# Perceiver megakernel: both products of the self-attention's values in one step, right ahead of the context's weighted values

## The chip, the cores and the metric

The kernel runs on one core of a Trainium2 chip. The metric is the device time of one execution in microseconds (us). The kernel before takes 2138.94 us (median of 3 runs, 2138.63 to 2139.02).

TensorE (PE) does the matrix products into PSUM, VectorE (DVE) and ScalarE (ACT) read PSUM and do the elementwise work and reductions, GpSimd (POOL) works on SBUF alone, and SyncE (SP) issues nearly all DMAs. Each engine takes its instructions in order, and an instruction that waits holds up what stands behind it.

## The reference, cut to what matters

The input is x (32 batches x 64 rows x 256) and a context (32 x 1601 x 256). Two layers follow each other, each of cross attention, a mixer and a feed-forward part, each with a layer norm ahead and a residual sum behind:

```
x = x + L0_xattn(ln(x), ctx)     # a mean of the context, two matmuls
x = x + L0_attn(ln(x))           # self-attention over 64 rows, 16 heads of 16, with a slope per head
x = x + L0_ffn(ln(x))            # shared expert + 2 of 8 routed experts
x = x + L1_xattn(ln(x), ctx)     # 16 heads over 1601 context rows: nearly all of the work
x = x + L1_attn(ln(x))           # convolution, a recurrent unit, a feed-forward part
x = x + L1_ffn(ln(x))            # ternary weights, quantised activations
```

The change is in L0_attn:

```
scores = q @ k.T / sqrt(16) + slopes * dist
attn   = softmax(scores)         # 64 x 64 for each batch and head
ctx    = attn @ v
out    = ctx @ Wo.T + bo
```

## The kernel before, in words

**Tiles.** The 2048 rows of x are 16 tiles of 128 rows (two batches each), taken in the order 1, 2, ..., 15, 0. The first layers (the three L0 steps) of a tile are one Python generator, `layer0`; the second cross attention is the main loop; what comes behind it for a tile is another generator, `tail`.

**The main loop** runs over `g`, 13 iterations for each tile: 12 pieces of 512 context columns (2 batches x 2 halves of the heads x 3 pieces) and one for the 65 columns left in each batch. For each `g` the engines' instructions are written in this order, which is also the order in which each engine's queue gets them:

1. `column_scores(g)`: the scores (PE lines 816 and 822, tile `s`), and their exp on ACT into `pt` (line 828).
2. `values(g + 4)`: values of the context (PE line 234 into `vps`, copied by DVE into `vau`, line 758). Once for each piece row also `maxima_rows` (`tpm`, line 797).
3. `run(g, 0)`: the planned generators' steps that were announced with `yield ACT`.
4. `row_scores(g + 5)`: scores by rows (PE line 774, tile `r`) and their maxima on DVE (line 781).
5. `weighted(g)`: the context's weighted values (PE line 846, tile `o` from `pt` and `vau`), matmuls of 128 rows and 32 columns each.
6. `keys(g + 6)`: keys (PE line 234 into `kps`, copied by ACT into `kt`, line 741).
7. `run(g, 1)`: the planned generators' other steps.

**The planner.** `Steps` holds a generator with a start, an end and a number of steps. With `place=3` it takes at most one step at each place of an iteration, and only as far as its due time allows; a step announced with `yield ACT` goes to place 0, any other to place 1. The first layers of the tiles 4 to 15 and 0 are planned in this way, two tiles overlapping. Tile 3 has `place=2` (any step at either place), tile 2 runs beside the start of the loop, and tile 1 is issued ahead of the loop, step by step from a list.

**The self-attention's end in `layer0`.** After the softmax, with the weights in `s`, there are three steps, all at place 0 of successive iterations:

- first: `weights(0)` turns four pairs of heads by TensorE transposes (line 416, PSUM tile `tpp`), and `weights_out` copies them to `pT` on ACT (line 421);
- second: `weights(1)`, then `summed_values(0, pT)`: eight matmuls of 128 rows and 32 columns (line 428; 16 records in the trace) into a PSUM tile `o0`, and ACT's copy with a bias to `oT` (line 431); then the second copy into `pT`, whose tag has one buffer;
- third: `summed_values(1, pT)`.

The output projection `wo` (line 234) and the residual sum follow at place 1, then `tp_c`, `su`, `sv`, `lg` and `so` of the shared expert.

**PSUM.** `s` and `r` share two tiles of two banks each, so `r` waits for the exps and the next `s` for the maxima. All other matmuls (`vps`, `kps`, `tpm`, and every step of the generators) take turns in three buffers of one bank (`mm_tile`), in the order in which they are written.

Of the kernel before, what the change touches and what calls it, by code (L numbers as in the profile page):

```python
# [15 lines left out]
P = 128  # L16
# [28 lines left out]
def perceiver_kernel(ctx: ExitStack, tc: tile.TileContext, a: dict, out: bass.AP):  # L45
# [14 lines left out]


    ACT = "ACT"

    def sc_tile(name):
        return ps_sc.tile([P, 2, 512], F32, tag="sc", name=name)
# [225 lines left out]
    def layer0(ti, csum, k=0, soon=False):  # L291
        def tile_(shape, tag, name):
            return front_tile(shape, tag, f"{name}_{ti}", k)
# [16 lines left out]
        xn = normalised(tile_([P, D], "xn", "xn_a"), m)  # L310
        yield ACT
        xT = transposed(xn, f"a{ti}", SECOND["xT"] if k else "xT")
# [21 lines left out]
        xn = normalised(tile_([P, D], "xn", "xn_b"), m)  # L334
        yield ACT


        xT = transposed(xn, f"b{ti}", SECOND["xT"] if k else "xT")
        yield ACT
        q_ps = mm_tile([P, 2, P], f"q0_{ti}")  # L340
# [11 lines left out]
        kbd = [tile_([P, 2, 4, S], "kbd", f"kbd{oc}") for oc in range(2)]  # L352
        for oc in range(2):
            nc.gpsimd.tensor_tensor(  # L354
                kbd[oc], kT[:, oc, :].rearrange("p (b k) -> p b k", b=2).unsqueeze(2).to_broadcast([P, 2, 4, S]),
                mask4.unsqueeze(1).unsqueeze(3).to_broadcast([P, 2, 4, S]), ALU.mult)
        yield ACT
        v_ps = mm_tile([P, 2, P], f"v0_{ti}")
# [40 lines left out]
        else:  # L399
            nc.gpsimd.tensor_tensor(s, s, mx.unsqueeze(2).to_broadcast([P, H, S]), ALU.subtract)  # L400
            yield
            yield ACT
            nc.scalar.activation(s, s, AF.Exp)
# [4 lines left out]
            yield  # L408
            yield ACT
        oT = tile_([P, 2, P], "oT", "oT")  # L410

        def weights(oc):
            t = mm_tile([P, 4, P], f"tpp_{ti}_{oc}")
            for j in range(4):
                hp = 4 * oc + j
                nc.tensor.transpose(t[:, j, :], s[:, 2 * hp:2 * hp + 2, :].rearrange("p h k -> p (h k)"), ident)
            return t

        def weights_out(oc, t):
            pT = tile_([P, 4, P], "pT", f"pT{oc}")  # L420
            nc.scalar.copy(pT, t)
            return pT

        def summed_values(oc, pT):
            o_ps = mm_tile([P, P], f"o0_{ti}_{oc}")
            for b in range(2):
                for i in range(4):
                    nc.tensor.matmul(o_ps[32 * i:32 * i + 32, b * S:(b + 1) * S],
                                     lhsT=vbd[k][:, b, 4 * oc + i].rearrange("p h d -> p (h d)"),
                                     rhs=pT[:, i, b * S:(b + 1) * S], start=True, stop=True)  # L430
            nc.scalar.activation(oT[:, oc, :], o_ps, AF.Identity, bias=chv[:, oc, BV:BV + 1])

        pT = weights_out(0, weights(0))
        yield ACT
        t = weights(1)
        summed_values(0, pT)
        pT = weights_out(1, t)
        yield ACT
        summed_values(1, pT)
        yield  # L440
        o = mm_tile([P, D], f"wo_{ti}")
        mm2(o, lambda c: oT[:, c, :], lambda c: w_o[:, c, :])
# [250 lines left out]
    def scanned(g):  # L693

        pos, p = divmod(g, NU)
        return (pos, 4 * pos + (p - 1) // NP, (p - 1) % NP) if p else (pos, None, None)
# [86 lines left out]
    def maxima(h):  # L783

        hf = halves[h]
        ng = small.tile([P, 4], F32, tag="ng", name=f"ng_{hf.name}")
        nc.vector.tensor_reduce(ng, wholes[hf.pos].mx[:, :, h % 4, :], AX.X, ALU.max, negate=True)
        m = mxp[h % 2]
        nc.vector.tensor_copy(m[:, :, 0], ng)
        nc.vector.tensor_tensor(ng, ng, m[:, :, 0], ALU.subtract)  # L790
        nc.vector.tensor_copy(m[:, :, 1], ng)
        nc.vector.tensor_tensor(m[:, :, 2], ng, m[:, :, 1], ALU.subtract)
# [38 lines left out]
    def weighted(g):  # L831

        pos, h, k = split(g)
        w = wholes[pos]
        first, last = g % NU == 0, g % NU == NU - 1
        if first:
            w.o = o_tile([P, 4, 2, S], f"o1_{w.ti}")
        v, pts = vau[g % 5], w.pt.pop(g)
        kr = TAIL if h is None else P
        for j in range(4):  # L840
            q = j if h is None else h % 4
            for m in range(2):
                for c in range(4):
                    hd = 4 * m + c

                    nc.tensor.matmul(w.o[32 * c:32 * c + 32, q, m, :], lhsT=v[:kr, j, 17 * hd:17 * hd + 32],  # L846
                                     rhs=pts[m][:kr, c // 2, j, c % 2 * S:c % 2 * S + S],
                                     start=(m == 0 and (first and j == 0 or h is None and j == 3)), stop=(m == 1 and (last and j == 3 or h is None and j == 2)))
        if h is None:
            w.osb = work.tile([P, 2, 4, S], F32, tag="osb", name=f"osb_{w.ti}", bufs=1)  # L850
            nc.vector.tensor_copy(w.osb[:, :, 0:3], w.o[:, 0:3].rearrange("p q m s -> p m q s"))
        elif last:
            nc.vector.tensor_copy(w.osb[:, :, 3], w.o[:, 3])
# [307 lines left out]
    class Steps:  # L1161
# [14 lines left out]
                    self.gen = None  # L1176

        def run(self, t, place):
            at = place if self.place == 2 else self.place
            if self.place == 3:  # L1180
                if (self.kind == ACT) != (place == 0):
                    return
                at = place
            if at == place:
                now = t + (0.5 * place if self.place >= 2 else 0)
                while self.gen is not None and self.done * (self.t1 - self.t0) <= (now - self.t0) * self.n:
                    self.step()
                    if self.place == 3:
                        break
# [85 lines left out]
    with tc.manual_schedule(engines={ET.PE, ET.DVE, ET.Activation, ET.Pool}):  # L1275
        ahead, beside, summing = Steps(first()), Steps(first_layer(1, 1)), Steps(early_sums())

        def besides():
            if 1 in csums:
                beside.step()  # L1280

        def scored():
            row_scores(scores.pop(0))

        scores = list(range(5))
        do = {"a": ahead.step, "b": besides, "s": summing.step, "r": scored, "w": late_weights, "m": lambda: maxima(0),
              "t": lambda: maxima_rows(0)}
        do |= {f"k{g}": lambda g=g: keys(g) for g in range(6)} | {f"v{g}": lambda g=g: values(g) for g in range(3)}

        for what in """a a a a k1 a a k2 a a s s k3 k0 a a a a s s s s a k4 a v0 v1 a a a s s s s s s b a b a b a b a s w  # L1290
                    a s s a a a b a a s s s r b r b s s s r k5 b r m s s s r v2 t""".split():
            do[what]()
        if beside.gen is not None:
            plan.insert(0, Steps(beside.gen, 0, 4, 28 - beside.done, 2))
        planned(biased(), 3, 5, 2, 1)
        if summing.gen is not None:
            plan.insert(0, Steps(summing.gen, 0, 4.5, 37 - summing.done, 0))
        planned(all_ternary(), 5, 23, 24, 2)

        def run(t, place):  # L1300
            for s in [s for s in plan if s.t0 <= t]:
                s.run(t, place)
                if t >= s.t1 and t < NU * NT - 1:
                    s.all()
                if s.gen is None:
                    plan.remove(s)

        for g in range(NU * NT):
            pos, p = divmod(g, NU)
            if pos + 1 < NT:  # L1310
                if p == 0:
                    wholes[pos + 1].rest = load_rest(order[pos + 1])
                if p in (2, 9):
                    load_batch(2 * pos + 2 + p // 8)
            column_scores(g)
            if g == 0:
                values(3)
            if g + 4 < NU * NT:
                values(g + 4)
            if p == 1 and pos:  # L1320
                normalise(pos - 1)
            if g + 4 < NU * NT and scanned(g + 4)[2] == NP - 1:
                maxima_rows(scanned(g + 4)[1])
            run(g, 0)
            if g + 5 < NU * NT:
                row_scores(g + 5)
                if scanned(g + 5)[2] == NP - 1:
                    maxima(scanned(g + 5)[1])
            weighted(g)
            if p == NU - 1:  # L1330
                gathered(pos)
            if g + 6 < NU * NT:
                keys(g + 6)
            if p == 1 and pos:
                x4[pos - 1] = projected(pos - 1)
            run(g, 1)
        normalise(NT - 1)
        x4[NT - 1] = projected(NT - 1)
        plan.append(Steps(second_layer(NT - 1)))
        while plan:  # L1340
            for s in list(plan):
                s.step()
                if s.gen is None:
                    plan.remove(s)
# [46 lines left out]
```

## Time and profile before

| what | value |
|---|---|
| median of 3 runs | 2138.94 us |
| the profiled execution, its time | 2137.64 us |
| its span | 2135.9 us |
| TensorE busy | 2020.8 us (95%) |
| VectorE, ScalarE, GpSimd busy | 1296.5, 906.4, 324.1 us |
| products of values, L428 | 512 records, 37.1 to 1563.6 us |
| transposes, L416 | 128 records, 35.0 to 1554.9 us |
| copies pT, L421, on ACT | 32, median 585 ns |
| copies oT, L431, on ACT | 32, median 367 ns |

A matmul in float32 is two records in the trace. In a timeline, a line is a run of like instructions: start, length in us, engine, line of the kernel, operation, out<-in, sizes and count, and in brackets the idle time before it and what ended it. Ends of matmuls are modelled and reach into the next run, so the time that a run holds TensorE is read from its start to the start of the next. In the chain a line is start, length, and what ran. In the answer on one line of the kernel, a row names what TensorE sat idle for, the sum in us and how many times.

### The profile page before, as it was taken

Reading aid. Unit: us, or ns where it says so; the run is one execution under the profiler, and the core shown is the slowest. Engines: PE = TensorE matmul, PEld = TensorE weight load, DVE = VectorE, ACT = ScalarE, POOL = GpSimd, SP = SyncE. Lnnn points to the kernel's source line nnn. Section 1 sums busy time; section 2 is a strip of 40 time slices with the busy share of each in tenths; the row PEclk is TensorE's granted clock in tenths of the full one; section 3 lists DMA queues with packets and bytes.
Section 4 is the critical chain, followed back from the end, with each engine's and each line's share of the span. In section 5 each row is a group of like instructions: output and inputs, shape, how many; then the busy total and the mean of one; then the engine's idle time right before and its main releaser. Section 6 shows DMA issues by size and latency. Waiting matters only on the chain.

```text
span 2135.9 us, 69475 instructions
## 1 busy us (share of the span) xinstructions
PE 2020.8 (95%) x31675; PEld 1468.0 (69%) x31675; DVE 1296.5 (61%) x2607; ACT 906.4 (42%) x1402; POOL 324.1 (15%) x538
## 2 busy tenths in 40 slices
PE   5899999999999999999999999999999999999964
PEld 3566677777776777777777777767776666676753
DVE  4555756666656666665667666566666656565544
ACT  4344444543546343444544434343433334334332
POOL 2121211111111111111111111111200111000011
PEclk9899999999999999999999999999999999999986
DMA  8334322221222212112211101111111111101000
GB/s 301 101 107 149 111 93 95 81 84 36 95 80 86 89 43 76 38 58 72 70 59 38 48 9 45 38 38 43 45 45 34 50 38 35 55 2 45 2 14 5
DMA packets 54638, 136.37 MB, mean 64 GB/s; under 512 B 13318, under 2 KB 34760, under 8 KB 54344
## 3 DMA queue, kind: packets, MB, share of 16 engines
q1 hardware_dynamic: 53784, 131.12, 18.1%
q8 instruction: 248, 4.06, 0.8%
q10 hardware_dynamic: 560, 0.81, 0.1%
q14 instruction: 46, 0.38, 0.1%
HBM read 125.60 MB, written 6.32 MB: 62 GB/s over the span
## 4 chain that ended last, share of the span: by engine, by line
PE 86%; DVE 8%; ACT 3%; issue 2%; DMA 1%; POOL 1%; SPq 0%; POOLq 0%; DVEq 0%; ACTq 0%
PE vps L234 18%; PE kps L234 16%; PE r L774 10%; PE o L846 9%; PE s L822 8%; PE ff L234 4%; PE s L816 3%; DVE mx L781 3%; PE ffo L997 2%; PE q L234 1%; PE wo L234 1%; ACT pt L828 1%; DVE vau L758 1%; PE hg L948 1%; PE h L1046 1%
## 5 line engine op out<-in xcount | busy, mean ns | idle before, releaser
L781 DVE TENSOR_REDUCE mx<-r 128x2 f32<-128x1024 f32 x384 | 451.8, 1219 | 123.1 <-PE r L774 122.8
L828 ACT ACTIVATE pt<-s 128x1024 f32<-128x1024 f32 (+1 forms) x416 | 403.1, 1020 | 276.5 <-PE s L822 276.3
L741 ACT ACTIVATE kt<-kps,chv 128x512 f32<-128x512 f32 x192 | 131.9, 687 | 641.6 <-PE kps L234 641.6
L234 PE MATMUL kps<-ctxT,w_L_xattn_WkT 128*128 128x512 f32 x768 | 384.2, 623 | 11.8 <-DMA ctxT<-ctxT 11.8
L234 PE MATMUL vps<-w_L_xattn_WvT,ctxT 128*128 128x128 f32 x3072 | 393.5, 281 | 1.3 <-DVE y L923 0.7
L234 PEld LDWEIGHTS vps<-w_L_xattn_WvT,ctxT 128*128 128x128 f32 x3072 | 357.4, 191 | 26.4 <-issue 3.8
L758 DVE COPY vau<-vps 128x512 f32<-128x512 f32 (+1 forms) x208 | 143.3, 689 | 355.6 <-PE vps L234 355.3
L846 PEld LDWEIGHTS o<-pt,vau 128*32 128x32 f32 (+1 forms) x13312 | 195.6, 110 | 150.8 <-issue 138.2
L846 PE MATMUL o<-pt,vau 128*32 128x64 f32 (+1 forms) x13312 | 230.0, 221 | 5.3 <-ACT pt L828 5.2
L774 PE MATMUL r<-kt,qbd 32*128 32x512 f32 x1536 | 227.6, 645 | 2.8 <-DVE mx L781 2.0
L234 PEld LDWEIGHTS kps<-ctxT,w_L_xattn_WkT 128*128 128x128 f32 x768 | 131.4, 191 | 124.1 <-issue 106.9
L822 PEld LDWEIGHTS s<-qbd,kt 32*128 32x128 f32 x6144 | 205.4, 186 | 3.0
L822 PE MATMUL s<-qbd,kt 32*128 32x128 f32 x6144 | 206.8, 270 | 0.0
L774 PEld LDWEIGHTS r<-kt,qbd 32*128 32x128 f32 x1536 | 65.5, 184 | 39.8 <-issue 19.0
L816 PE MATMUL s<-neg,onesb 3*128 3x512 bf16 x768 | 80.8, 384 | 5.1 <-DVE mx L781 4.1
L816 PEld LDWEIGHTS <-onesb 3*128 3x128 bf16 x768 | 21.0, 90 | 93.5 <-issue 91.9
L276 ACT ACTIVATE part<-part 128x1601 f32<-128x1601 f32 x48 | 74.1, 1544 | 0.2
L234 PE MATMUL ff<-nT,w_fg 128*128 128x128 f32 x384 | 51.7, 287 | 1.0 <-ACT nT L984 1.0
L234 PEld LDWEIGHTS ff<-nT,w_fg 128*128 128x128 f32 x384 | 47.9, 200 | 1.9 <-ACT nT L984 1.8
L354 POOL TENSOR_TENSOR kbd<-kT,mask 128x512 f32<-128x512 f32 x32 | 32.6, 1041 | 108.0 <-ACT kT L347 108.0
L234 PE MATMUL ff<-nT,w_fv 128*128 128x128 f32 x384 | 48.9, 278 | 0.0
L400 POOL TENSOR_TENSOR s<-s,mx 128x1024 f32<-128x1024 f32 x15 | 28.6, 1904 | 118.6 <-DVE mx L384 118.2
(339 smaller groups left out, 2444.5 us busy)
## 6 DMA issues: line engine op xcount, KB each, us to landing
ctxT<-ctxT SPq DMA_DIRECT2D x31, 1601.0 KB
part<-ctxT SPq DMA_DIRECT2D x60, 800.5 KB
od<-osb SPq DMA_DIRECT2D x16, 256.0 KB
rest<-ctxT SPq DMA_DIRECT2D x32, 65.0 KB
x<-x SPq DMA_DIRECT2D x16, 128.0 KB
rs<-od SPq DMA_DIRECT2D x32, 64.0 KB
og<-od SPq DMA_DIRECT2D x32, 64.0 KB
out<-x SPq DMA_DIRECT2D x16, 128.0 KB
```

Of the source, the lines that this page charges most:

```text
L234: nc.tensor.matmul(o, lhsT=lhsT(c), rhs=rhs(c), start=(c == 0), stop=(c == 1))
L276: nc.scalar.activation(parts[j], parts[j], AF.Copy, accum_out=csum[:, c, 2 * i + b:2 * i + b + 1])
L354: nc.gpsimd.tensor_tensor(kbd[oc], kT[:, oc, :].rearrange("p (b k) -> p b k", b=2).unsqueeze(2).to_broadcast([P, 2, 4, S]), mask4.unsqueez ...
L741: nc.scalar.activation(kt, o, AF.Identity, bias=chv[:, hf.oc, BK2:BK2 + 1])
L758: nc.vector.tensor_copy(v[:kr, :, 0:VW - 16].rearrange("p k (h d) -> p k h d", d=17)[:, :, :, 0:16], o[:kr].rearrange("p k (h d) -> p k h ...
L774: nc.tensor.matmul(o, lhsT=qbd[r, q % 2, q // 2].rearrange("p h q -> p (h q)"), rhs=w.kt[r, q, :] if h is None else halves[h].kt[k][r, :], ...
L781: nc.vector.tensor_reduce(w.mx[:, 2 * m:2 * m + 2, h % 4, k], ps[m], AX.X, ALU.max)
L816: nc.tensor.matmul(o, lhsT=onesb[r, :], rhs=halves[h].neg[r, :].unsqueeze(1).to_broadcast([3, 4, P]), start=True, stop=False)
L822: nc.tensor.matmul(ps[i // 2][:kr, i % 2, j * P:(j + 1) * P], lhsT=w.kt[r, j, :] if h is None else halves[h].kt[k][r, j * P:(j + 1) * P], ...
L828: nc.scalar.activation(pt[:kr].rearrange("p i k c -> p i (k c)"), ps[m][:kr], AF.Exp)
L846: nc.tensor.matmul(w.o[32 * c:32 * c + 32, q, m, :], lhsT=v[:kr, j, 17 * hd:17 * hd + 32], rhs=pts[m][:kr, c // 2, j, c % 2 * S:c % 2 * S ...
L997: nc.tensor.matmul(o, lhsT=m[:, f, :], rhs=w_fo[:, f, :], start=(f == 0), stop=(f == NF - 1))
```

## The change

Both products move into one step of their own, behind both steps of transposes. A new kind of announcement, `COL`, has its step run at a new place, 0.5, between `row_scores` (with `maxima`) and `weighted`. Generators planned with `place=2` have no place 0.5 and take the step at place 0 or 1. The second copy of the weights no longer shares the buffer of the first: it takes one of the two buffers of the tag `kbd`, which also hold the masked keys and, later, the routed experts' weights.

```
-            pT = tile_([P, 4, P], "pT", f"pT{oc}")
+            pT = tile_([P, 4, P], ("pT", "kbd")[oc], f"pT{oc}")
...
-        pT = weights_out(0, weights(0))
-        yield ACT
-        t = weights(1)
-        summed_values(0, pT)
-        pT = weights_out(1, t)
-        yield ACT
-        summed_values(1, pT)
+        pT = [weights_out(0, weights(0))]
+        yield ACT
+        pT.append(weights_out(1, weights(1)))
+        yield COL
+        for oc in range(2):
+            summed_values(oc, pT[oc])
         yield
...
         def run(self, t, place):
-            at = place if self.place == 2 else self.place
+            at = place if self.place == 2 and place != 0.5 else self.place
             if self.place == 3:
-                if (self.kind == ACT) != (place == 0):
+                if {ACT: 0, COL: 0.5}.get(self.kind, 1) != place:
                     return
                 at = place
...
                     maxima(scanned(g + 5)[1])
+            run(g, 0.5)
             weighted(g)
```

More of the change, by code (lines that the diff above doesn't have):

```diff
@@ L62, in perceiver_kernel @@
     ACT = "ACT"
+    COL = "COL"
     def sc_tile(name):
```

## The prediction

> **What bounds the kernel now.** The page was read first: busy times and the rows of 40 slices, then the chain.
>
> ```profile
> PE 2020.8 (95%) x31675; PEld 1468.0 (69%) x31675; DVE 1296.5 (61%) x2607; ACT 906.4 (42%) x1402; POOL 324.1 (15%) x538
> PE 86%; DVE 8%; ACT 3%; issue 2%; DMA 1%; POOL 1%; SPq 0%; POOLq 0%; DVEq 0%; ACTq 0%
> ```
>
> TensorE is busy 95% of the span and carries 86% of the chain. The busy times by stretch say where it idles:
>
> ```profile
> 120.00:1560.00 1440.00, 1415.81 (x22903) 1035.92 (x22902) 903.78 (x1797) 652.82 (x1006) 239.87 (x369) 1.00 0.20 67
> ```
>
> Between 120 and 1560 us, where all but three tiles' first layers run, it is busy 1415.81 of 1440 us at a granted clock of 1.00. So the change is worth what it does to TensorE's own queue, read from start to start in the timeline. Below is tile 15: first the iteration with its second group of transposes and its first product of values, then the next one with its second product.
>
> ```profile
> 1441.09 0.60 PE L416 MATMUL tpp<-ident,s 128*128 128x128 f32 x4
> 1441.62 0.43 PE L428 MATMUL o<-pT,vbd 128*32 128x64 f32 x16
> 1441.98 1.14 PE L774 MATMUL r<-kt,qbd 32*128 32x512 f32 x8
> 1443.05 1.10 PE L846 MATMUL o<-pt,vau 128*32 128x64 f32 x64
> 1444.08 1.98 PE L234 MATMUL kps<-ctxT,w_L_xattn_WkT 128*128 128x512 f32 x4
> ...
> 1449.10 0.22 PE L797 MATMUL tpm<-identb,mxp 128*128 128x128 bf16 x1
> 1449.25 0.43 PE L428 MATMUL o<-pT,vbd 128*32 128x64 f32 x16
> 1449.61 1.14 PE L774 MATMUL r<-kt,qbd 32*128 32x512 f32 x8
> ```
>
> What to see: a product (16 matmul records, each with a weight load that moves with it) holds the queue 0.36 us from its start to that of the row scores r. The context's weighted values (L846) have the same shape, 128x64 out of weights of 128*32, and hold it 1.03 us for 64 records, 0.016 us each. A product alone pays 0.022 us a record, as a short run pays the change into r each time.
>
> **The change, part by part.** Durations are of the profiled execution: span 2135.9 us, its time 2137.64 us, 1.3 us under the median of 2138.94 us.
>
> *Thirteen steady tiles (4 to 15, and 0).* In the changed kernel's order of instructions both products stand between r and L846, in the iteration of the second transposes. They leave two places.
> First place: transposes to product is 0.53 us, and transposes straight to r takes the same (a tile's first transposes, 1324.53 to 1325.06), so 0.36 us goes. Second place: from tpm to product 0.15 us, from tpm to r 0.14 us (1571.80 to 1571.94): another 0.36 us goes. Added: 32 records ahead of 64 of their own shape. L846 without its exit (0.15 us, the gap between its last start and the next line's) is 0.88 us for 63 steps, so 32 steps cost 0.45 us; r to a product should cost what r to L846 does, 1.07 us. Net 0.45 - 0.72 = -0.27 us, times 13 = **-3.5 us**. Bounds: 0, if the merged run keeps 0.36 us a product, and -0.36 us a tile, if one product rode along free. I take the row of the same shape in the same place.
> In seven of the 13, a step of full 128x128 size (tp_a in six, tp_b in one) stands right behind the second product. From the last start of the context's value product (vps) to the first of a product it is 0.20 us in the trace, to a full-size step 0.11 us; the dearer entry goes: 7 x 0.09 = **-0.6 us**.
>
> *Waits that go.* Beyond the 0.53 us, the first product starts late by 0.73 us in tiles 8 and 0, 0.20 in tiles 5 and 13, 0.09 in tiles 10 and 12; the second by 0.19 and 0.10 in tiles 9 and 10; tp_a behind it is late by 0.28, 0.41, 0.18, 0.28 in tiles 6, 9, 11, 14. What they wait for, from the answer on the product's line after 120 us:
>
> ```profile
>   DVE rr L953: 2.9, 4
>   DVE vau L758: 2.3, 6
> ```
>
> (TensorE and its weight loads each counted.) Both are readers of an older tile in the three shared PSUM buffers. Behind r the products start 1.07 us later, when those readers are through, and a product no longer pushes tp_a onto the buffer that vau is being copied from. Sum 3.5 us, less 0.1 each in tiles 8 and 0 for the next point: **-3.3 us**; bounds 0 (they return at another step) and -3.5.
>
> *The wait that is added.* The second product now needs pT1, whose transposes are in the same iteration.
>
> ```profile
> 1439.37 1.94 ACT L828 ACTIVATE pt<-s 128x1024 f32<-128x1024 f32 x2 [0.60 <-PE s L822]
> 1442.12 0.37 ACT L431 ACTIVATE oT<-o,chv 128x128 f32<-128x128 f32 x1 [0.80 <-PE o L428]
> 1442.38 0.58 ACT L421 COPY pT<-tpp 128x512 f32<-128x512 f32 x1
> ```
>
> Today pT1 stands behind oT0 on ACT; after the change it stands ahead of it, and ACT is idle 0.80 us there. The transposes end at 1441.69; pT1 would run 1441.75 to 1442.33. The second product is due 0.53 + 1.07 + 0.22 us after 1441.09, at 1442.91: 0.5 us in hand. Behind a late one L846, keys and the next s would stand. ACT is later than that in tiles 8 and 0 (a tanh of L952 ahead: 0.1 us) and in tile 9.
> Tile 9: the second exp ends at 790.01 only, and r cannot pass it, so its first place gives back nothing; with a Square ahead of pT1 I read 0.3 us above the formula. The exps also bind where little is left between values and r: behind a lone tpm, r takes longer,
>
> ```profile
> 1571.94 1.25 PE L774 MATMUL r<-kt,qbd 32*128 32x512 f32 x8
> ```
>
> 0.12 us above its 1.14. Tiles 7, 15 and 0 become such: 0.36. Together **+0.7 us**.
>
> *The first three tiles.* Tile 1 lies on the chain, where TensorE is idle and latency counts:
>
> ```profile
> 37.18 0.41 PE o L428 x16
> 37.60 0.37 ACT oT L431
> 37.97 0.48 ACT pT L421
> 38.50 0.43 PE o L428 x16
> ```
>
> pT1 no longer waits for the buffer of pT0 and for oT0. Transposes end at 37.18, pT1 runs 37.25 to 37.83, the second product starts at 37.87 instead of 38.50: -0.6. Tile 2: the product's wait for pT0 (105.55 to 106.06) leaves the path, 0.24 us of product comes in behind keys: -0.3. Tile 3: transposes to xat fall from 0.95 us (174.12 to 175.07) to 0.44, 0.24 comes in behind the next values: -0.3. **-1.2 us**; bounds -0.6 and -1.5.
>
> *At nothing.* ACT runs the same copies in another order; in tiles 4, 7 and 10 a part sum (L276, 1.53 us) stands between pT1 and oT0, covered by L846 and keys (1.03 + 1.92 us) before the output projection wants oT. POOL's second kbd write now waits for the previous tile's second product instead of its scores; it follows 10 us or more later (275.2 to 285.5 at the closest). On SP the first four w13 loads move behind a rest, a context load and an output; they wait for the last tile's product near 1557 instead of issuing at 1510.25, are wanted at 1633.9, and the next issue behind them is at 1575.70. The steps after the product (wo, tp_c, su, lg, so) come one iteration earlier in most tiles. Their own instructions are the same, but they meet other tiles' steps. No row prices that; iterations with three or more tiles behind the value product fall from 85 to 80 in the order, single waits of this kind are 0.2 to 0.5 us: bounds -1.5 and +2, taken as 0.
>
> **Sum:** -3.5 - 0.6 - 3.3 + 0.7 - 1.2 = -7.9 us. 2137.64 becomes 2129.7; against the median, 2138.94 - 7.9 = **2131.0 us**, 0.37% faster. About 0.2% (4.3 us) can be told from no change here.
>
> **The rivals.**
> *The waits move elsewhere.* Buffers stay three, and the later steps meet new neighbours; then the 3.3 goes and up to 2 comes: -4.6 to -2.6, 2134 to 2136. For: a third tile behind values is still there 80 times. Against: the removed ones sit at the product itself. 18%.
> *The merged run keeps the price of two single ones.* 32 records cost 0.72, the steady gain is nil: -7.9 + 3.5 = -4.4, 2134.5. Against: L846's 64 records in 1.03 us. 10%. [...]
> *Slower: pT1 late.* The product waits in order, with L846 behind it. If one more ACT task of a part sum's length (1.53 us) ran ahead of pT1 in each of the 13 tiles, it would cost 1.53 - 0.5 = 1.0 us a tile against a gain of about 0.55 (the 3.5, 0.6 and 3.3 over 13): +6, 2137.64 - 1.2 + 0.7 + 6 = 2143 in the profiled execution, 2144 by the median. It decides from 1.05 us of delay on. Against: in the changed order part sums stand behind pT1, and only L952 and Square come ahead, in few tiles. 8%.
> *The change doesn't do what it says*, the products being held to a later iteration by the planner's pace: all 13 stand in the iteration of their transposes, so it has no chance.
> New neighbours that also remove waits: 4%.
>
> **How the numbers follow.** The sum as told has 60%, its own range 2127.5 to 2134.5. The bounds added up reach from -11.1 to about +1.5, 2127.8 to 2140.4; the range 2127 to 2138.5 leaves out the late pT1 and the ends. Faster by over 0.2% (under 2134.7): nearly all of the 60, the 4, half of the 10 and half of the 18, less a little for what was not seen: 0.75. Same: 0.16. Slower 0.09.
>
> **What would show it.** After the change: L428 as one run of 32 records between r and L846, together 1.5 us; transposes to r 0.53 us; no wait of L428 for rr or vau; pT1 ahead of oT0 on ACT, and the product waiting for pT1 only in tiles 8, 9 and 0; the start of tile 1's projection 0.6 us earlier; TensorE busy a few us less. Wrong would be: r to L428 far above 1.07 us, waits for pT in most tiles, or new waits at tp, su or wo for vau that add up to more than 3 us.

## The result and the profile after

| | before | after |
|---|---|---|
| median | 2138.79 us (2137.12 to 2139.61, 6 runs) | 2127.99 us (2126.34 to 2129.98, 6 runs) |
| ratio, with its 95% interval | | 0.9949 (0.9940 to 0.9959) |
| span of the profiled execution | 2135.9 us | 2125.2 us |

The change makes the kernel 0.51% faster: 10.8 us by the medians, 10.7 us by the spans of the two profiled executions. The forecast was 7.9 us. Lines of the kernel after are numbered two higher than before up to the product's step, and one higher from there on: the product is L430, the transposes L418, the copies pT L423 and oT L433, r L775, the weighted values L847. In most of the experiments the lines behind the product's step are 6 or 7 higher still; a tile's name tells which step a row is.

The page of the kernel after, busy times and the chain by engine:

```profile
PE 2014.4 (95%) x31659; PEld 1468.2 (69%) x31675; DVE 1298.1 (61%) x2607; ACT 906.4 (43%) x1402; POOL 325.2 (15%) x538
PE 86%; DVE 8%; ACT 2%; issue 1%; DMA 1%; POOL 1%; SPq 0%; POOLq 0%; DVEq 0%; ACTq 0%
```

The busy times by stretch, the same stretch as before (length, then busy time and count of TensorE, its weight loads, DVE, ACT and POOL; granted clock; DMA share; GB/s):

```profile
120.00:1560.00 1440.00, 1420.06 (x23087) 1043.11 (x23094) 912.71 (x1814) 657.65 (x1012) 240.79 (x371) 1.00 0.20 67
```

TensorE is still what bounds the kernel. In the same 1440 us it is busy 4.25 us more and gets through 184 matmul records more (23087 against 22903), at the same granted clock of 1.00. The gain is in TensorE's queue, as the forecast said, and shows as more work done in the stretch.

Tile 15 in the timeline of the kernel after, TensorE:

```profile
1430.34 0.60 PE L418 MATMUL tpp<-ident,s 128*128 128x128 f32 x4
1430.87 1.14 PE L775 MATMUL r<-kt,qbd 32*128 32x512 f32 x8
1431.94 0.65 PE L430 MATMUL o<-pT,vbd 128*32 128x64 f32 x32
1432.41 1.08 PE L847 MATMUL o<-pt,vau 128*32 128x64 f32 x64
1433.42 1.12 PE L236 MATMUL kps<-ctxT,w_L_xattn_WkT 128*128 128x512 f32 x2
```

From start to start: transposes to r 0.53 us, r to the product 1.07, the product's 32 records 0.47, the weighted values 1.01. Before, the two products held the queue 0.36 us each and the weighted values 1.03.

ACT in the same iteration:

```profile
1428.63 1.94 ACT L829 ACTIVATE pt<-s 128x1024 f32<-128x1024 f32 x2 [0.60 <-PE s L823]
1430.98 0.58 ACT L423 COPY pT<-tpp 128x512 f32<-128x512 f32 x1 [0.41 <-PE tpp L418]
1432.44 0.62 ACT L433 ACTIVATE oT<-o,chv 128x128 f32<-128x128 f32 x2 [0.88 <-PE o L430]
```

The second pT now stands ahead of both oT copies and ends at 1431.56, 0.38 us before the joined run starts.

What TensorE waited for between 120 and 1560 us (sum in us, times, longest). The main rows of before that are gone or smaller after:

```profile
PE o L428 <- DVE rr L953: 1.2, 2, 0.6
PE q L234 <- ACT kT L347: 0.7, 1, 0.7
PE tp_a L218 <- DVE vau L758: 0.7, 3, 0.3
PE tp_b L218 <- DVE vau L758: 0.5, 1, 0.5
PE tp_b L218 <- ACT xT_d L224: 0.5, 2, 0.2
PE v L362 <- ACT xT_c L224: 0.5, 1, 0.5
PE o L428 <- DVE vau L758: 0.3, 1, 0.3
```

and the rows of after that are larger than before, new, or what is left of those above:

```profile
PE r L775 <- ACT pt L829: 3.8, 9, 0.5
PE vps L236 <- issue: 0.6, 1, 0.6
PE tp_a L220 <- DVE vau L759: 0.3, 1, 0.3
```

The product of values waits for nothing any more in this view. Three of the rows that went (q, v, and tp_b for xT_d) are not waits of the product or of the step behind it: they belong to steps further down, and the forecast had no term for them. Three more rows of before, of 0.3 to 0.5 us each, went as well, and two small ones came: wo for oT, 0.3 us, and tp_c for xn_c, 0.2 us, once each.

Where along the run the time goes is read by comparing the two timelines iteration by iteration, each from the start of its first matmul to the start of the next iteration's. The shift of after against before is -1.14 us at the end of iteration 17 (the first three tiles), -11.66 at the end of iteration 161 (the thirteen steady tiles), still -11.66 at iteration 203, and -10.66 at the end. So the steady tiles gave 10.5 us, the first ones 1.1, and the last stretch took 1.0 back. That last loss is the clock's: the granted clock was 0.83 and 0.74 between 2034 and 2042 us (the last section).

### The profile page after: what moved, and what is told of

The parts are those of the page before. It is cut to its first block, busy times and chain, and to the rows that moved or that the text cites. A ratio compares the mean times of both kernels' runs of the same rounds, so it can differ in the third digit from the quotient of the medians.

```text
span 2125.2 us, 69448 instructions
## 1 busy us (share of the span) xinstructions
PE 2014.4 (95%) x31659; PEld 1468.2 (69%) x31675; DVE 1298.1 (61%) x2607; ACT 906.4 (43%) x1402; POOL 325.2 (15%) x538
## 4 chain that ended last, share of the span: by engine, by line
PE 86%; DVE 8%; ACT 2%; issue 1%; DMA 1%; POOL 1%; SPq 0%; POOLq 0%; DVEq 0%; ACTq 0%
PE vps L236 18%; PE kps L236 16%; PE r L775 10%; PE o L847 9%; PE s L823 8%; PE ff L236 4%; PE s L817 3%; DVE mx L782 3%; PE ffo L998 2%; PE q L236 1%; PE wo L236 1%; ACT pt L829 1%; PE hg L949 1%; PE h L1047 1%; PE gps L633 1%
## 5 line engine op out<-in xcount | busy, mean ns | idle before, releaser
L847 PEld LDWEIGHTS o<-pt,vau 128*32 128x32 f32 (+1 forms) x13312 | 196.6, 110 | 141.6 <-issue 129.1
L847 PE MATMUL o<-pt,vau 128*32 128x64 f32 (+1 forms) x13312 | 230.4, 221 | 5.3 <-ACT pt L829 5.2
L775 PE MATMUL r<-kt,qbd 32*128 32x512 f32 x1536 | 227.8, 645 | 2.8 <-DVE mx L782 2.0
L775 PEld LDWEIGHTS r<-kt,qbd 32*128 32x128 f32 x1536 | 65.6, 184 | 41.4 <-issue 21.7
L236 PEld LDWEIGHTS ff<-nT,w_fv 128*128 128x128 f32 x384 | 46.1, 194 | 0.0
```

What stands on the lines that cost most here:

```text
L236: nc.tensor.matmul(o, lhsT=lhsT(c), rhs=rhs(c), start=(c == 0), stop=(c == 1))
L775: nc.tensor.matmul(o, lhsT=qbd[r, q % 2, q // 2].rearrange("p h q -> p (h q)"), rhs=w.kt[r, q, :] if h is None else halves[h].kt[k][r, :], ...
```

## The experiments

In all of them but the one that moves the place itself, the tiles 1, 2 and 3 are as in the change; diffs are against the changed kernel, and in those with an `else:` the lines shown stand in it, for the tiles 4 to 15 and 0. Two kinds of number are given. The median goes with a ratio to the kernel before, timed along with the experiment. The steady shift is worked out from the traces: the shift against before at the end of iteration 161 less that at the end of iteration 17. It leaves out the start, where profiled executions differ by up to 4.4 us ahead of the steady tiles; in the change it is -10.52 us. It still holds differences of single executions: iterations 113 and 139, whose order is the same in the change and in the run with the place one step later, differ there by 0.4 and 0.2 us. The expectations call the account of the forecast, with the iteration of the later steps as a cause of its own, A; their other letters are rivals that lay the gain on fewer causes.

### One step at place 0: the joined products, without the new place

```
-            yield COL
+            yield ACT
             for oc in range(2):
                 summed_values(oc, pT[oc])
```

The joined products run at place 0 in the iteration after the second transposes, where the second product was; all later steps keep their old iterations.

> Both products in one step, but at place 0 (ahead of the row scores) of the iteration behind the second transposes, so that the later steps stay in the iterations they had before; tiles 4 to 15 and 0 only, the first three tiles as in the change. Theory A (the gain of 10.8 us is about 1 us from the first three tiles, 6 us from the place of the products and 4 us from the later steps coming one iteration earlier): one of two changes of shape remains, -0.36 + 0.22 us a tile, 13 x -0.14 = -1.8, the waits at the first product go, -2, and 1 from the first tiles: about 2134. Theory B (all of it is the place between row scores and weighted values): only the first tiles' 1 us is left, 2138. Theory C (all of it is the earlier iteration): 2138 too.

Measured: 2139.04 us, ratio 0.9994 (0.9985 to 1.0004): no gain, about 5 us above the expected 2134; steady shift +0.80 us. The miss is in the second place. The first place gave back its 0.36 us in nearly all tiles, and 1.04 in tiles 8 and 0, as expected; but the joined run held the queue far longer than expected, for instance in tile 15, in this run's timeline:

```profile
1452.00 0.22 PE L804 MATMUL tpm<-identb,mxp 128*128 128x128 bf16 x1
1452.15 0.43 PE L430 MATMUL o<-pT,vbd 128*32 128x64 f32 x16
1453.04 0.43 PE L430 MATMUL o<-pT,vbd 128*32 128x64 f32 x16 [0.46 <-DVE vau L765]
1453.40 1.14 PE L781 MATMUL r<-kt,qbd 32*128 32x512 f32 x8
```

1.25 us from the first product to r, where one product alone held 0.36. The second product takes a second of the three PSUM buffers at once, close behind the values' own. In four tiles (6, 7, 14, 15) it waits until DVE has copied `vau` out of one, in two (9, 10) for ACT, and in three others the step behind it waits for `oT`. Where nothing waits (tiles 5, 13 and 0) the joined run holds 0.58 to 0.59 us, as expected. The waits view of this run gives the sums (one more row is 0.3 us for `qT_i`):

```profile
PE o L430 <- DVE vau L765: 1.3, 4, 0.5
PE o L430 <- ACT h L1047: 0.9, 1, 0.9
PE tp_a L220 <- ACT oT L433: 0.5, 2, 0.3
PE tp_b L220 <- ACT oT L433: 0.3, 1, 0.3
```

What follows: joining the products was worth nothing here, where no other long step stands between the values and them. I had counted the buffers for the new place only.

### The new place alone: the products apart, each behind r

```
             pT.append(weights_out(1, weights(1)))
+            yield "COL0"
+            summed_values(0, pT[0])
             yield COL
-            for oc in range(2):
-                summed_values(oc, pT[oc])
+            summed_values(1, pT[1])
```

with, in the planner,

```
                     self.kind = next(self.gen)
+                    if self.kind in ("ACT0", "COL0"):
+                        self.kind, self.done = self.kind[:3], self.done - 1
```

so that the added step does not count towards the planner's pace. Each product keeps its old iteration and stands behind r there.

> Both products at the new place ahead of the weighted values, but each in the iteration in which it was before, so that the later steps stay where they were; first three tiles as in the change. Theory A: the place without the earlier iteration, 2138.8 - 1 - 6 = 2132 (2131 to 2133). Theory B: nothing is lost against the change, 2128. Theory C: 2138.

Measured: 2133.76 us, ratio 0.9975 (0.9965 to 0.9984), 0.8 us above the expected 2131 to 2133; steady shift -5.59 us. In it 1.6 us was lost in iteration 47, where the order is the same as before and the granted clock fell to 0.72 and 0.85 (last section), so about -7.2 us is the edit's. Tile 15's first product in this run's timeline:

```profile
1438.66 0.43 PE L430 MATMUL o<-pT,vbd 128*32 128x64 f32 x16
1438.91 1.08 PE L854 MATMUL o<-pt,vau 128*32 128x64 f32 x64
```

Each product holds the queue 0.25 us, against 0.36 at its old place, and none of them waits in this trace between 120 us and the last product. The place pays without any joining: two runs of 0.25 and one run of 0.47 cost nearly the same.

### The change with its later steps held

```
             for oc in range(2):
                 summed_values(oc, pT[oc])
+            yield "ACT0"
```

An empty step behind the products (not counted either, by the same two lines) keeps `wo` and all that follows in the iterations of the kernel before.

> The change with one thing taken back: for tiles 4 to 15 and 0 an empty step behind the products holds the output projection and all later steps in the iterations they had before. Theory A: 4 us of the gain go, 2132 (2131 to 2133), and the trace differs from that of the change only where those later steps stand. Theory B: 2128, no difference. Theory C: 2138, nearly all of the gain goes.

Measured: 2130.94 us, ratio 0.9964 (0.9951 to 0.9977), just under the expected 2131 to 2133; steady shift -6.78 us, against -10.52 in the change. The later steps' earlier iteration is worth 3.7 us. It can be followed to the place. Of the thirteen steady tiles, seven have their later steps one iteration earlier in the change (4, 6, 8, 9, 11, 14, 0). Comparing the change with this run over just those iterations gives -0.77, -0.70, -1.08, +0.09, -0.73, -0.70 and +0.02 us: -3.9 together; the rest of the steady stretch makes up +0.1. Tile 8 shows how. The timeline of this run, TensorE:

```profile
712.91 0.38 PE L220 MATMUL tp_g<-ident,xs_g 128*128 128x128 f32 x2
713.13 1.06 PE L236 MATMUL su<-xT_c,w_L_ffn_sw1T 128*128 128x128 f32 x8
714.02 1.06 PE L236 MATMUL sv<-xT_c,w_L_ffn_sw3T 128*128 128x128 f32 x8
714.92 1.06 PE L236 MATMUL k<-xT_b,w_L_attn_WkT 128*128 128x128 f32 x8
716.69 1.16 PE L236 MATMUL q<-xT_b,w_L_attn_WqT 128*128 128x128 f32 x8 [0.72 <-ACT kT L349]
```

and the same iteration in the change:

```profile
713.37 0.38 PE L220 MATMUL tp_g<-ident,xs_g 128*128 128x128 f32 x2
713.59 1.06 PE L236 MATMUL k<-xT_b,w_L_attn_WkT 128*128 128x128 f32 x8
714.49 1.06 PE L236 MATMUL q<-xT_b,w_L_attn_WqT 128*128 128x128 f32 x8
715.47 1.14 PE L775 MATMUL r<-kt,qbd 32*128 32x512 f32 x8
```

With su and sv of the one tile ahead of k and q of the next, five matmul groups follow each other through three PSUM buffers, and q stands for 0.72 us. In the change su and sv are an iteration earlier, among lighter neighbours, and k to q falls from 1.77 us to 0.90. In tiles 6 and 14 the gain is `tp_c`, which stood 0.63 us behind two long `ff` steps and `tp_d`, and an `s` that falls from 1.28 to 0.99 us; in tile 11 it is `tp_c` too (0.89 to 0.37).

### The products at place 0, in the transposes' own iteration

```
             pT.append(weights_out(1, weights(1)))
-            yield COL
             for oc in range(2):
                 summed_values(oc, pT[oc])
+            yield COL
```

The later steps are as early as in the change; only the place differs.

> Both products directly behind the second transposes at place 0, in the same iteration, so that the later steps come as early as in the change, without the new place; first three tiles as in the change. The second product then waits for pT1: transposes to row scores 1.66 us where the change has 0.53 there and 0.45 behind: +0.7 us a tile against the change. Theory A: 2128 + 13 x 0.7 = 2137, up to 2139 with the waits for buffers that return. Theory B: 2138 or above. Theory C (the iteration alone): 2128 to 2130.

Measured: 2139.29 us, ratio 0.9992 (0.9983 to 1.0001), at the upper end of what was expected: the whole gain is gone; steady shift -0.64 us, 9.9 more than in the change, 0.76 us a tile. On TensorE the products wait for pT (3.8 us in 11 waits) and for rr (1.2 us in 2), and in tile 15 transposes to r is 1.64 us, 0.53 to the first product, 0.75 to the second and 0.36 to r. Without r's 1.07 us in between, the second copy has not been made.

### One buffer for both copies: a late pT1

```
-            pT.append(weights_out(1, weights(1)))
+            t = weights(1)
             yield COL
-            for oc in range(2):
-                summed_values(oc, pT[oc])
+            summed_values(0, pT[0])
+            summed_values(1, weights_out(1, t))
```

with the second copy in the buffer of the first, so that it has to wait for the first product.

> The change without the second buffer: for tiles 4 to 15 and 0 the second copy of the weights goes into the buffer of the first again and so is written between the two products. This prices a late pT1. If TensorE really stands still for it (theory A): the second product starts 1.12 us behind the first instead of 0.22, +0.9 us a tile, 13 x 0.9 = 11.7: 2139.7. If the wait is covered by the maxima on VectorE that the next scores need anyway (rival): 2128 to 2130.

Measured: 2144.54 us, ratio 1.0026 (1.0015 to 1.0036), slower than before the change; steady shift +5.99 us, 16.5 more than in the change. Its timeline in tile 15:

```profile
1447.49 0.43 PE L430 MATMUL o<-pT,vbd 128*32 128x64 f32 x16
1448.89 0.43 PE L430 MATMUL o<-pT,vbd 128*32 128x64 f32 x16 [0.96 <-ACT pT L423]
1449.13 1.08 PE L853 MATMUL o<-pt,vau 128*32 128x64 f32 x64
```

The two products hold the queue 1.64 us instead of 0.47, 1.17 more. I had expected 0.9: on ACT the copy also stands behind the first oT (1447.99, then pT at 1448.26). Thirteen times 1.17 is 15.2 of the 16.5 us; most of the rest is in iteration 73, where the weighted values hold 1.86 us and keys 2.14 (793.36 to 797.36), for 1.01 and 1.82 in the change, rows stretched as in the fall of the clock in the last section. The rival that a late pT1 would make the kernel slower was therefore a true mechanism with about the price given, though what makes the copy late here is the buffer and not another task of ACT. In the change it did not happen because the second buffer lets the copy be made while r runs.

### The place one step later

```
-            run(g, 0.5)
             weighted(g)
+            run(g, 0.5)
```

> The new place moved behind the weighted values, ahead of keys: the same neighbours of the same shape, 1 us more for pT1. Theory A (what counts is the neighbour of the same shape and the iteration): within 1 us of the change, 2127 to 2128.5, the product's waits for pT1 gone. Rival (it must stand ahead of the weighted values, since keys then wait for a buffer that pT1 or oT holds): above 2129, with new idle time ahead of keys.

Measured: 2127.52 us, ratio 0.9947 (0.9932 to 0.9962): the same as the change within the intervals; steady shift -11.08 us against -10.52. In tile 15 the weighted values hold 0.92 us and the products 0.56, the other way round 0.47 and 1.01: 1.48 both times. No product of the steady tiles in the change waits for pT, so there was nothing for the later place to save. Nor does keys wait behind the products in this trace, so the rival that they must stand ahead of the weighted values falls.

### The products issued twice

```
-            for b in range(2):
+            for b in [0, 1] * (1 if ti in (1, 2, 3) else 2):
```

Every product of the steady tiles is computed twice into the same PSUM tile, 64 records in place of 32.

> The change with every product of tiles 4 to 15 and 0 issued twice (the same matmuls into the same place, only more work): 64 records instead of 32 ahead of the weighted values. It prices the records themselves. By the row of the weighted values (14 ns a record, 0.45 us for 32): 13 x 0.45 = +5.9, 2133.9. By the price of a product alone (0.72 us): +9.4, 2137.4. [...]

Measured: 2134.81 us, ratio 0.9987 (0.9977 to 0.9996), 0.9 us above the lower of the two prices expected, 2133.9, and 2.6 below the other. Tile 15 in its timeline:

```profile
1436.89 1.14 PE L775 MATMUL r<-kt,qbd 32*128 32x512 f32 x8
1437.96 1.10 PE L430 MATMUL o<-pT,vbd 128*32 128x64 f32 x64
1438.88 1.08 PE L847 MATMUL o<-pt,vau 128*32 128x64 f32 x64
```

0.92 us in place of 0.47, in every steady tile: 32 records more cost 0.45 us, 14 ns each. Over 13 tiles that is 5.9 of the 6.8 us between the two medians; the steady shift is larger, because in the profiled execution the weighted values and keys are stretched in iterations 47 and 138 as well, to 1.81 and 2.75 us and to 1.76 and 2.80, for 1.03 and 1.92, 1.6 us each time; iterations 113 and 139 give 1.1 of that back.

## Why the prediction was right, and where its size was off

The direction, the bound and the way were right; the size was off by 2.9 us (2127.99 against 2131.0), inside the range given for the likeliest case, near its lower end. That it is inside is partly luck: one term was missed by more than its bound, and a loss at the end that nobody foresaw hid a part of it. By its own steps, against the profiled execution's -10.66:

| step of the forecast | forecast | measured |
|---|---|---|
| thirteen steady tiles -3.5, full-size step behind the second product -0.6, waits that go -3.3, the wait that is added +0.7 | -6.7 | -6.78, with the later steps held |
| first three tiles | -1.2 | -1.14 |
| at nothing: later steps one iteration earlier | 0 | -3.7 |
| not in the forecast: the end of the run | | +1.0 |

*Thirteen steady tiles.* Row for row as worked out: 0.53, 1.07, 0.47 and 1.01 us for the expected 0.53, 1.07, 0.45 and 1.03 in tile 15. Taking 32 records from the row of the same shape in the same place was what made this right; the experiment with doubled products gives 0.45 for 32 more. The rival that the joined run keeps the price of two single ones (0.72 us) falls with that. In tile 15's joined run a record takes 14 ns on average, 28 ns a matmul of the program at two records each; the first four records start between 1431.94 and 1431.97, the next four between 1432.02 and 1432.05.

The first four terms are measured together, as -6.78; that this is so near their sum is closer than the traces allow to tell, since single iterations of the same order differ by 0.2 to 0.4 us between two of them.

*Waits that go.* They did go: no wait of the product for rr or vau is left. They went because of the place, as argued: with the products apart behind r there is none either, and with the products joined at place 0 the waits for `vau` come back (1.3 us on the product), and others with them.

*The wait that is added.* The reserve of about 0.5 us held. In tile 15 pT1 ends 0.38 us ahead of the joined run, and the second product, which is the one that needs it, starts about 0.25 us into the run: 0.6 us. The waits of 0.1 us for pT1 that I foresaw in tiles 8 and 0 did not come, nor one in tile 9: the joined run is 0.47 us in all three. In tiles 8 and 0 it was close: there pT1 ends 0.12 us after the joined run has started, 0.1 us ahead of the second product. In tile 9 the exp holds r itself, as foreseen, and that iteration alone became 0.45 us longer with the later steps held (1.3 in the change, where the projection has come into it). The row of r in the change:

```profile
783.26 1.11 PE L775 MATMUL r<-ktr,qbd 32*128 32x65 f32 x28 [0.47 <-ACT pt L829]
```

*The first three tiles.* Tile 1 in the chain of the kernel after:

```profile
37.34 0.59 ACT pT L423
37.94 0.04 issue
37.98 0.43 PE o L430 x16
38.41 1.20 PE wo L236 x4
```

The second product starts at 37.98 instead of 38.50: 0.52 us, where the forecast said 0.6 (37.87). The transposes themselves started 0.07 us later in this execution (36.62 against 36.55), so from there it is 0.59. Tiles 2 and 3 were forecast at -0.6: from the start of iteration 1 to the end of iteration 17 all eight traces that have the change in these tiles shift by -0.62 or -0.63 us against before.

*At nothing.* This is the step that failed: the price of the later steps' earlier iteration. I saw that the later steps come an iteration earlier, had a count for it (iterations with three or more tiles behind the value product fall from 85 to 80), bounded it between -1.5 and +2 us, and took 0. It was -3.7, beyond the bound. The count was the right sign to look at and the price was too small: the waits that went are of 0.3 to 0.9 us (k to q 0.87, `tp_c` 0.3 to 0.5, `s` 0.3), and several of them stood in rows of before's waits that I had not put against the new order: q for kT 0.7, v for xT_c 0.5, tp_b for xT_d 0.5. The rival that the waits move elsewhere had the right object and the wrong sign; that new neighbours also remove waits, which is what happened, stood in the forecast with 4%.

Without the clock's fall at the end, the gain in the profiled execution would have been 11.7 us. How many of the timed executions had that fall isn't known.

## What to carry to other kernels

Where one engine's queue is the bound and its steps share a few PSUM buffers, what stands directly ahead of a step can matter more than how long the step is: here the same 32 records gained nothing at one place (2139.04 us, steady shift +0.80) and 7 us at another (steady shift -6.78), a microsecond of other work further on. When a step that ends a chain of steps moves up, price its followers as well: take each wait that the trace shows on them and on their neighbours, and ask of each whether the two still meet in the new order. Here a short run took its time per record from a run of the same shape next to it, not from itself alone at another place: 32 records held the queue 0.47 us ahead of the weighted values, where 16 alone had held 0.36.

## What the hardware showed that I had not expected

*Short falls of TensorE's clock after small waits, in some executions only.* In iteration 47 r is held twice by the exp. In the run with the products apart, the busy times by stretch (columns as above) say what happened next:

```profile
542.00:546.00 4.00, 3.52 (x95) 3.07 (x94) 2.47 (x5) 1.85 (x4) 0.79 (x2) 0.72 0.92 307
546.00:550.00 4.00, 4.00 (x57) 2.20 (x56) 1.86 (x4) 1.13 (x2) 2.98 (x2) 0.85 0.26 107
```

and its timeline, which rows were stretched:

```profile
541.64 0.44 PE L782 MATMUL r<-ktr,qbd 32*128 32x65 f32 x4 [0.42 <-ACT pt L836]
542.56 1.11 PE L782 MATMUL r<-ktr,qbd 32*128 32x65 f32 x28 [0.48 <-ACT pt L836]
543.60 1.84 PE L854 MATMUL o<-pt,vau 128*32 128x64 f32 x64
545.37 2.86 PE L236 MATMUL kps<-ctxT,w_L_xattn_WkT 128*128 128x512 f32 x4
```

The granted clock fell to 0.72 and 0.85, which is 4 x 0.28 + 4 x 0.15 = 1.7 us of lost clock, and the weighted values and keys took 1.77 and 2.79 us instead of 1.03 and 1.92. The kernel after has the same waits at 538.45 and 539.37, and its clock stays at 1.00. TensorE was idle here for about 0.4 to 0.5 us at a time in both; what sets off a fall, these runs do not show.

The change met one such fall at its end. Its busy times by stretch there:

```profile
2034.00:2038.00 4.00, 2.22 (x81) 1.87 (x80) 3.44 (x6) 1.94 (x2) 0.08 (x1) 0.83 0.01 4
2038.00:2042.00 4.00, 2.75 (x60) 2.14 (x52) 0.00 (x0) 1.47 (x2) 0.00 (x0) 0.74 0.01 2
```

In stretches of half a microsecond the granted clock is 0.66 from 2036.5 on, 0.50 in each of the six from 2037.0 to 2040.0, and 0.93 from 2040.0 on: 1.7 us of lost clock here too. In the kernel before the same work, some 11 us later, runs at 1.00 until 2054. That takes back about 1.5 us, of which 0.5 are won again behind it. Between iterations 203 and 207 the profiled executions of four of the experiments lose 1.4 to 2.0 us against before too, some of it won again behind (the products apart, the later steps held, place 0 in the transposes' iteration, the place one step later), and those of the other three nothing. Events like these may account for part of the 2 to 8 us by which executions of one kernel differ; that was not tried.

*Narrow matmuls.* Records with weights of 128 rows and 32 columns and 64 moving columns followed each other at 14 ns in a long run: 0.45 us for the step from 32 to 64 of them in the experiment with doubled products. The mean hides that they start in fours, closely together, as the times of tile 15's joined run above show.
